# Running channel attention and SwiGLU in one loop, and moving a tile's closing sum ahead of the next row maxima

## The chip, the core and the metric

The kernel runs on one core of one Trainium2 chip. A core has five engines that each work through their own queue of instructions in order: TensorE (PE in the profile, with its weight loads as PEld), VectorE (DVE), ScalarE (ACT), GpSimd (POOL) and SyncE (SP), which here only issues transfers. They meet only at semaphores: an instruction that waits holds up everything behind it on its own engine. The metric is the device time of one execution in microseconds (us).

## The reference, cut to what matters

A decoder of four layers with three sublayers each. Only the first three sublayers are touched. `x` is 64 sequences of 64 tokens with 256 features, 4096 tokens in all; each sublayer is added to its input and normalized.

```python
x = layernorm(x + attn(x))            # first:  16 heads of 16, one key/value head, causal
x = layernorm(x + xattn(x, ctx, ctx)) # second: attention over channels
x = layernorm(x + ffn(x))             # third:  SwiGLU, hidden size 704

def xattn(q, k, v):                   # per sequence
    scaled = einsum('bsd,bse->bde', q, k) / 16
    attn = softmax(scaled, axis=1)
    return einsum('bde,bse->bsd', attn, v)

def ffn(x):                           # weights are integers: W = (wq - 128) * scale
    return (silu(x @ Wgate.T) * (x @ Wup.T)) @ Wdown.T
```

The other nine sublayers (attentions, a recurrence, quantized feed-forwards) follow in the same way and are not changed.

## The kernel before

**Tiles.** `x` stays on the core, in eight groups of four tiles of 128 tokens (two sequences a tile): `self.X[g][:, t, :]`. The context is there twice, by token (`cn`) and turned (`self.CT[g]`). Every product is in float32; the profile lists such a product as two MATMUL instructions.

**Order.** Each sublayer is a method called from `run`; a framework places the instructions of each engine and writes the semaphores. Inside `with self.tc.manual_schedule(engines=...)` the named engines keep the order in which the code issues their instructions; the other engines are placed freely. Weights come through a ring of eight buffers of 8 KB per partition (`self.weight`). PSUM, which holds the products, has eight banks, divided afresh by each sublayer.

**First sublayer, `l0_attn`.** A loop of 36 iterations over the 32 tiles, with the order of TensorE, ScalarE, VectorE and GpSimd written out. In iteration i:

- TensorE: the scores of tile i (`s`, onto a mask product), the values of tile i-3 (`ot`), one part of the next group's projections (`prepare`: turning, then keys and values, then two halves of the queries), the turned probabilities of tile i-2 (`pt`), and the output projection of tile i-3 (`o`, one PSUM bank).
- VectorE: the largest value of each row of tile i (`mx`), the subtraction, the row sums of tile i-1 (`sm`), their reciprocal, and then `ended` for tile i-4: add the output in PSUM to the input (`z`, line 605), and the statistics (606, 607). After a group's fourth tile `ended` also issues the reciprocal root, half on VectorE (228), half on GpSimd (230).
- GpSimd: the products of probabilities and reciprocals (565), and the input with bias for the next group (`xb`, 521).

**Second sublayer, `l0_xattn`.** A loop over 32 tiles; only TensorE's order is written out. Per tile: four score products on 64 rows each into a PSUM tile of two banks (`s`, three buffers), the largest values (686, 687), four exponentials that also give their sums (692), the reciprocal (696), the division folded into the values on GpSimd (`vt`, 702), and, two tiles later, four value products (712), the sum (713) and, for the fourth tile of a group, the layernorm, its last step on VectorE (267).

**Third sublayer, `l0_ffn`.** Integer weights are loaded into one ring buffer each and scaled into another (line 778). For each group: two transposes (`xt`), then six chunks of 128 hidden features (the last has 64): a gate and an up product of four MATMULs each (738), the SiLU on ScalarE (740), the product on VectorE (741); then for each of four tiles the down product over all six chunks (749), the sum (792), and at the end the layernorm. No engine's order is written out.

The SiLU and the exponential need different tables on ScalarE; the compiler puts an ACT_TABLE_LOAD in front of an activation whose table is not the one loaded.

Of the kernel before, what the change touches and what calls it, by code (L numbers as in the profile page):

```python
# [9 lines left out]
F32 = mybir.dt.float32  # L10
BF16 = mybir.dt.bfloat16
FP8 = mybir.dt.float8e4
I32 = mybir.dt.int32
# [5 lines left out]
P = 128  # L19
# [5 lines left out]
NEG_INF = -1.0e38  # L25
ROUND = 12582912.0
WCOLS = 2048
LAYERS = 8


class Linear:
# [164 lines left out]
class Decoder:  # L196
# [154 lines left out]
    def run(self, layers):  # L351
        tc, nc, ctx = self.tc, self.nc, self.ctx
        self.const = self.pool(ctx, "const", 1)
        self.smallp = self.pool(ctx, "small", 4)
        self.xpool = self.pool(ctx, "xpool", 1)
        self.ring = self.pool(ctx, "ring", 8)

        self.X, self.CT, self.l3_rows = [], [], []
        for g in range(self.n_groups):
            xg = self.xpool.tile([P, TG, D], F32, tag=f"x{g}", name=f"x{g}")  # L360
            self.load(xg, self.ins["x"][g * NTOK : (g + 1) * NTOK, :].rearrange("(t p) d -> p t d", p=P))
            self.X.append(xg)
# [86 lines left out]
    def l0_attn(self, ctx):  # L449
# [178 lines left out]
        with self.tc.manual_schedule(engines={E.PE, E.Activation, E.DVE, E.Pool}):  # L628
# [34 lines left out]
        self.load(cn, self.ins["ctx"][g * NTOK : (g + 1) * NTOK, :].rearrange("(t p) d -> p t d", p=P))  # L663
        return cn

    def l0_xattn(self, ctx):

        nc = self.nc  # L670
        wk = ctx.enter_context(self.tc.tile_pool(name="l0x", bufs=2, reuse_waits="tile"))
# [3 lines left out]
        groups, state = {}, {}  # L675

        def scores(g, t):
            x, cn = self.X[g], groups[g][0]
            ps = self.psum.tile([P, 2, 2, D], F32, tag="s", name="s", bufs=3)
            for e in range(2):  # L680
                for b in range(2):
                    nc.tensor.matmul(
# [6 lines left out]
            for b in range(2):  # L689
                for e in range(2):  # L690
                    i = 2 * b + e
                    nc.scalar.activation(
                        p[:, b, e, :], ps[:, b, e, :], AF.Exp, bias=nb[:, i : i + 1], scale=scale,
                        accum_out=sm[:, i : i + 1],
                    )
            nc.vector.reciprocal(sm, sm)
# [3 lines left out]
            sums = sm.rearrange("p (b e) -> p b e", b=2)  # L700
            for b in range(2):
                nc.gpsimd.tensor_tensor(
                    vt[:, b], src[:, b], sums[:, b].unsqueeze(2).broadcast_to([P, 2, S]), ALU.mult
                )
            return p, vt

        def values(g, t, p, vt):
            x, z = self.X[g], groups[g][1]
            ps = self.bank("o", tag="o", bufs=2)
            for e in range(2):  # L710
                for b in range(2):
                    nc.tensor.matmul(ps[half(b), :D], vt[:, b, e, :], p[:, b, e, :], start=e == 0, stop=e == 1)
            nc.vector.tensor_tensor(z[:, t, :], ps[:, :D], x[:, t, :], ALU.add)
            if t == TG - 1:
                self.layernorm(x, z)

        tiles = [(g, t) for g in range(self.n_groups) for t in range(TG)]
        n = len(tiles)
        with self.tc.manual_schedule(engines={mybir.EngineType.PE}):
            for i in range(n + 2):  # L720
                if i < n:
                    g, t = tiles[i]
                    if t == 0:
                        groups[g] = cns[g], wk.tile([P, TG, D], F32, tag="z", name="z")
                    state[i] = scores(g, t)
                if i >= 2:
                    values(*tiles[i - 2], *state.pop(i - 2))

    def gated(self, wk, xt, w_gate, w_up, n_hid):

        nc = self.nc
        hs = []
        for h0 in range(0, n_hid, P):
            n = min(P, n_hid - h0)
            pg, pu = self.bank("gate"), self.bank("up")
            for ps, w in ((pg, w_gate), (pu, w_up)):
                for c in range(2):
                    nc.tensor.matmul(ps[:n], w(c, h0, n), xt[:, c, :], start=c == 0, stop=c == 1)
            h = wk.tile([P, NTOK], F32, tag="hid", name="hid", bufs=10)
            nc.scalar.activation(h[:n], pg[:n], AF.Silu)  # L740
            nc.vector.tensor_tensor(h[:n], h[:n], pu[:n], ALU.mult)
            hs.append((h, n))
        return hs

    def down(self, hs, w_down, t):

        ps = self.bank("down", tag="acc", bufs=2)
        for i, (h, n) in enumerate(hs):
            self.nc.tensor.matmul(
                ps[:, :D], h[:n, t * P : (t + 1) * P], w_down(i, n), start=i == 0, stop=i == len(hs) - 1  # L750
            )
        return ps[:, :D]

    def l0_ffn(self, ctx):

        nc, ins = self.nc, self.ins
        wk = self.pool(ctx, "l0f", 2)
        HID = 704
        ws = []
        for name, scale, n, parts in (  # L760
            ("l0_wg", "l0_sg", HID, 2),
            ("l0_wu", "l0_su", HID, 2),
            ("l0_wd", "l0_sd", D, 6),
        ):
            sc = self.spread(wk, scale, n)
            raw, w = self.weight(name + "_q", I32), self.weight(name)
            cols = parts * n
            full = ins[name].shape[0] // P
            r3 = raw[:, :cols].rearrange("p (c n) -> p c n", c=parts)
            w3 = w[:, :cols].rearrange("p (c n) -> p c n", c=parts)  # L770
            self.load(r3[:, :full, :], ins[name][: full * P, :].rearrange("(c p) n -> p c n", p=P))
            blocks = [(slice(0, P), c) for c in range(full)]
            if full < parts:
                rest = slice(0, ins[name].shape[0] - full * P)
                self.load(r3[rest, full, :], ins[name][full * P :, :])
                blocks.append((rest, full))
            for rows, c in blocks:
                nc.vector.scalar_tensor_tensor(
                    w3[rows, c, :], r3[rows, c, :], -128.0, sc[rows], ALU.add, ALU.mult
                )  # L780
            ws.append(w3)
        wg, wu, wd = ws
        for g in range(self.n_groups):
            x = self.X[g]
            xt = self.transposed(x, wk, "xt")
            hs = self.gated(
                wk, xt, lambda c, h, n: wg[:, c, h : h + n], lambda c, h, n: wu[:, c, h : h + n], HID
            )
            z = wk.tile([P, TG, D], F32, tag="z", name="z")
            for t in range(TG):  # L790
                ps = self.down(hs, lambda i, n: wd[:n, i, :], t)
                nc.vector.tensor_tensor(z[:, t, :], ps, x[:, t, :], ALU.add)
            self.layernorm(x, z)

    def l1_attn(self, ctx):

# [1367 lines left out]
```

## Time and profile before

| | |
|---|---|
| time, median of 3 runs | 4535.5 us (4533.63 to 4536.48) |
| time of the profiled execution | 4529.3 us |
| its span, first to last instruction | 4527.5 us |
| busy share of the span: PE, DVE, ACT, POOL | 91%, 69%, 42%, 33% |
| mean granted TensorE clock | 0.967 |
| first sublayer, by its first and last TensorE instruction | about 5 to 247 us |
| second sublayer | 247.3 to 355.7 us |
| seam between second and third, until the first gate and up products are done | 355.7 to 371.3 us |
| third sublayer, from there to its last product | 371.3 to 637.6 us |
| fourth sublayer starts | 637.6 us |

Each row of the views below gives an engine, a line of the kernel, the operation, and what it writes and reads by the program's names. In the list of instructions in order of time the first two columns are the start and the duration in us, and the square bracket is how long the engine sat idle before it and what ended that. The view by stretches gives for each the length, then each engine's busy time with its number of instructions, then the granted clock, the share of the transfer engines and GB/s. A busy TensorE is counted from the start of a MATMUL to its modelled end, which overlaps with the next, so the pace of its work is read from the distance between starts.

### The profile page before, as it was taken

The numbers are of one execution on the slowest core, as the hardware profiler recorded it, in microseconds if no ns is written. First come the engines' busy times: TensorE is split into PE (matmuls) and PEld (weight loads), VectorE is DVE, ScalarE is ACT, GpSimd is POOL, SyncE is SP. The second block draws the span as 40 slices with busy tenths as digits, with TensorE's granted clock in tenths as the row PEclk, the third lists the DMA queues.
The fourth block names the chain that finished last, engine by engine and source line by source line (L and its number), as shares of the span: only waits on it lengthen the run. The fifth ranks groups of instructions, "written<-read, shape, count | busy, mean of one in ns | idle before, by whom it ended". The sixth has DMA issues, their size and how long they took to land. (4 is left out here: it accounts for less than half of the span.)

```text
span 4527.5 us, 73819 instructions
## 1 busy us (share of the span) xinstructions
PE 4123.3 (91%) x28808; PEld 2661.1 (59%) x28808; DVE 3113.5 (69%) x6262; ACT 1920.5 (42%) x3552; POOL 1476.0 (33%) x1498
## 2 busy tenths in 40 slices
PE   7879997989988999849999999999979999999898
PEld 5544555666665555525666666666646666666566
DVE  6774235888775577767777777777757677777676
ACT  4551123767623566534444444444423332233344
POOL 3431011142331111105555555555523333333111
PEclk9999997999999999969999999999989999999999
DMA  4001011333300000011111111111220000000000
GB/s 129 3 1 47 1 35 37 60 82 70 80 1 21 1 0 1 10 47 24 29 29 24 29 29 24 29 29 24 57 68 10 10 10 10 10 10 13 7 16 17
DMA packets 99684, 128.25 MB, mean 28 GB/s; under 512 B 14916, under 2 KB 72452, under 8 KB 97928
## 3 DMA queue, kind: packets, MB, share of 16 engines
q1 hardware_dynamic: 99336, 123.53, 10.9%
q8 instruction: 228, 3.74, 0.3%
q14 instruction: 120, 0.98, 0.1%
HBM read 61.87 MB, written 19.42 MB: 18 GB/s over the span
## 5 line engine op out<-in xcount | busy, mean ns | idle before, releaser
L230 POOL TENSOR_TENSOR hrq<-hrq,neg_half 128x4 f32<-128x4 f32 x256 | 270.9, 1058 | 510.0 <-DVE hrq L228 509.9
L230 POOL TENSOR_TENSOR rstd<-rstd,neg_half 128x4 f32<-128x4 f32 (+1 forms) x168 | 148.3, 883 | 798.9 <-DVE rstd L228 713.4
L1003 DVE TENSOR_REDUCE mc<-sq 128x2 f32<-128x512 f32 x512 | 317.0, 681 | 61.1 <-PE sk L1001 60.7
L1009 ACT ACTIVATE e<-sk 128x512 f32<-128x512 f32 x512 | 265.1, 605 | 111.1 <-PE sk L1001 110.2
L230 POOL TENSOR_TENSOR hrk<-hrk,neg_half 128x4 f32<-128x4 f32 x160 | 187.9, 1175 | 290.8 <-DVE hrk L228 280.4
L998 PE MATMUL sq<-l1x 32*128 32x256 f32 x2048 | 273.9, 405 | 2.0 <-DVE mc L1003 2.0
L1505 PE MATMUL p<-l3a_wq,xt 128*128 128x512 f32 x512 | 244.4, 600 | 9.9 <-DVE v L217 9.9
L1001 PE MATMUL sk<-l1x 32*128 32x256 f32 x2048 | 251.5, 391 | 0.2 <-DMA l1x<-l1x_m 0.2
L1505 PE MATMUL p<-l3x_wq,xt 128*128 128x512 f32 x512 | 235.7, 603 | 14.1 <-DVE k L1814 14.0
L1505 PE MATMUL p<-l3a_wk,xt 128*128 128x512 f32 x512 | 247.1, 605 | 0.0
L998 PEld LDWEIGHTS sq<-l1x 32*128 32x128 f32 x2048 | 207.9, 194 | 54.8 <-issue 23.1
L1895 PE MATMUL acc<-l3x_wo,yt 128*128 128x256 f32 x1024 | 238.0, 385 | 0.7 <-ACT yt L215 0.7
L1505 PE MATMUL p<-l3a_wv,xt 128*128 128x512 f32 x512 | 234.4, 600 | 0.8 <-DVE k L217 0.4
L1712 PE MATMUL acc<-l3a_wproj,yt 128*128 128x256 f32 x1024 | 232.4, 380 | 0.0
L1712 PEld LDWEIGHTS acc<-l3a_wproj,yt 128*128 128x128 f32 x1024 | 194.7, 191 | 53.0 <-issue 29.2
L1895 PEld LDWEIGHTS acc<-l3x_wo,yt 128*128 128x128 f32 x1024 | 189.3, 190 | 28.3 <-ACT yt L215 0.9
L1001 PEld LDWEIGHTS sk<-l1x 32*128 32x128 f32 x2048 | 187.7, 186 | 6.9 <-issue 2.5
L1505 PEld LDWEIGHTS p<-l3x_wq,xt 128*128 128x128 f32 x512 | 96.7, 195 | 125.4 <-issue 115.1
L1696 POOL TENSOR_TENSOR hry<-hry,neg_half 128x8 f32<-128x8 f32 x64 | 106.2, 1660 | 192.9 <-DVE hry L1692 192.9
L1806 ACT ACTIVATE sq<-q 128x512 f32<-128x512 f32 x128 | 80.7, 630 | 205.4 <-DVE q L1814 153.1
L236 PEld LDWEIGHTS qT<-ident,q 128*128 128x128 f32 x1024 | 119.1, 141 | 77.5 <-issue 64.5
L236 PEld LDWEIGHTS pt<-ident,s 128*128 128x128 f32 x768 | 93.4, 144 | 105.8 <-issue 65.4
(374 smaller groups left out, 10227.9 us busy)
## 6 DMA issues: line engine op xcount, KB each, us to landing
vs<-v SPq DMA_DIRECT2D x320, 128.0 KB
x<-in_x SPq DMA_DIRECT2D x8, 512.0 KB
ct<-in_ctxT SPq DMA_DIRECT2D x8, 512.0 KB
cn<-in_ctx SPq DMA_DIRECT2D x8, 512.0 KB
l1x<-in_ctx SPq DMA_DIRECT2D x128, 32.0 KB
l1x_x<-x SPq DMA_DIRECT2D x8, 512.0 KB
l1x<-l1x_x SPq DMA_DIRECT2D x128, 32.0 KB
l1x_r<-r SPq DMA_DIRECT2D x128, 32.0 KB
```

Source lines behind the costliest of these rows:

```text
L230: nc.gpsimd.tensor_tensor(out, out, self.neg_half[:, :n], ALU.pow)
L236: self.nc.tensor.transpose(ps[:, j * P : (j + 1) * P], blk, self.ident)
L998: nc.tensor.matmul(ps[:, n, :], x_[rows, j, part], c_[rows, j, :], start=True, stop=True)
L1001: nc.tensor.matmul(ps[:, n, :], c_[rows, j, part], x_[rows, j, :], start=True, stop=True)
L1003: nc.vector.tensor_reduce(mc[new % 2][:, ra + k, 2 * j : 2 * j + 2], ps, AX.X, ALU.max, negate=True)
L1009: nc.scalar.activation(es[rb + k], ps, AF.Exp, scale=scale)
L1505: self.nc.tensor.matmul(ps, lhs(c), w(c, cols), start=c == 0, stop=c == 1 and bias is None)
L1696: nc.gpsimd.tensor_tensor(r, r, self.neg_half[:, :8], ALU.pow)
L1712: nc.tensor.matmul(acc[:, :D], yts[h % 2][:, h // 2, :], wp[n // 8][:, (n % 8) * D : (n % 8 + 1) * D], start=n == 0, stop=n == 15,)
L1806: nc.scalar.activation(sq, x, AF.Square)
L1895: nc.tensor.matmul(acc[:, :D], yts[h % 2][:, h // 2, :], wo[n // 8][:, (n % 8) * D : (n % 8 + 1) * D], start=n == 0, stop=n == 15,)
```

## The change

Two things change.

In `l0_attn`, `ended` for tile i-4 moves from behind the row sums of tile i-1 to the head of the iteration, in front of the scores and row maxima of tile i.

`l0_xattn`, `l0_ffn` and their helpers `gated` and `down` are replaced by one method, `l0_both`, with the order of all four compute engines written out. Its loop runs over 48 units, one per group and chunk of the third sublayer, with eight units ahead and two behind. Unit u issues the gate and up products of chunk u, the scores of a tile of the second sublayer (of the next group; in four of six units), the down products of chunk u-2 for all four tiles, and the values of the tile whose scores came two units earlier. Scores fall on units with u mod 6 = 4, 5, 0, 1 and values on u mod 6 = 0, 1, 2, 3; the next group's rows are turned at the end of units with u mod 6 = 5. Its statistics are taken tile by tile, and the normalization is applied on ScalarE instead of VectorE, one unit after the last sum. PSUM: `s` has one buffer of two banks instead of three, `o` one bank, gate, up and the turned rows share three, and the accumulators have two. Integer weights are scaled in place, so three ring buffers are taken instead of six.

```diff
@@ run
-            self.l0_attn, self.l0_xattn, self.l0_ffn, self.l1_attn, self.l1_both,
+            self.l0_attn, self.l0_both, self.l1_attn, self.l1_both,
@@ l0_attn
             for i in range(n + 4):
                 behind = ends.pop(0) if ends else None
+                if i >= 4:
+                    ended(*tiles[i - 4], state.pop((i - 4, "ps")))
                 if i < n:
...
                 if 3 <= i <= n + 2:
                     state[i - 3, "o"] = values(*tiles[i - 3], state.pop((i - 3, "pt")))
-                if i >= 4:
-                    ended(*tiles[i - 4], state.pop((i - 4, "ps")))
                 if parts:
                     parts.pop(0)()
@@ l0_both
-    def l0_xattn(self, ctx):
...
-    def gated(self, wk, xt, w_gate, w_up, n_hid):
...
-    def down(self, hs, w_down, t):
...
-    def l0_ffn(self, ctx):
...
+    def l0_both(self, ctx):
...
+            raw = self.weight(name, I32)
+            r3 = raw[:, : parts * n].rearrange("p (c n) -> p c n", c=parts)
+            w3 = raw.bitcast(F32)[:, : parts * n].rearrange("p (c n) -> p c n", c=parts)
...
+        def ended(g, z):
+            mv = state.pop((g, "mv"))
+            rstd, nb = self.small(TG, "rstd", bufs=4), self.small(TG, "nmr", bufs=4)
+            self.rsqrt(rstd, mv[:, :, 1], 1.0, 1e-5)
+            def apply():
+                nc.vector.scalar_tensor_tensor(nb, mv[:, :, 0], -1.0, rstd, ALU.mult, ALU.mult)
+                for i in range(TG):
+                    nc.scalar.activation(
+                        self.X[g][:, i, :], z[:, i, :], AF.Identity, bias=nb[:, i : i + 1], scale=rstd[:, i : i + 1]
+                    )
+            ends.append(apply)
+        def sums(g, t, z, ps):
...
+            nc.vector.tensor_tensor(z[:, t, :], ps, self.X[g][:, t, :], ALU.add)
+            nc.vector.bn_stats(st, z[:, t, :])
+            nc.vector.bn_aggr(state[g, "mv"][:, t, :], st)
...
         def scores(g, t):
...
-            ps = self.psum.tile([P, 2, 2, D], F32, tag="s", name="s", bufs=3)
+            ps = self.psum.tile([P, 2, 2, D], F32, tag="s", name="s", bufs=1)
...
+        def divided(g, t):
+            p, sm = state[g, t]
             nc.vector.reciprocal(sm, sm)
...
+        def values(g, t):
...
+            sums(g, t, z, ps[:, :D])
             if t == TG - 1:
-                self.layernorm(x, z)
+                ended(g, state.pop((g, "z")))
...
+        def turn(g):
+            xt = wk.tile([P, 2, NTOK], F32, tag="xt", name="xt")
+            for c, copy in enumerate((nc.scalar.copy, nc.vector.tensor_copy)):
+                ps = self.bank("xt", tag="gu", bufs=3)
+                for t in range(TG):
+                    nc.tensor.transpose(ps[:, t * P : (t + 1) * P], self.X[g][:, t, c * P : (c + 1) * P], self.ident)
+                copy(xt[:, c, :], ps)
...
+        def hidden(g, i):
+            pg, pu = self.bank("gate", tag="gu", bufs=3), self.bank("up", tag="gu", bufs=3)
...
+            nc.scalar.activation(h[:n], pg[:n], AF.Silu)
             nc.vector.tensor_tensor(h[:n], h[:n], pu[:n], ALU.mult)
...
+        def down(g, i):
...
+            for t in range(TG):
+                nc.tensor.matmul(
+                    state[g, "acc"][t // 2][:, t % 2, :], h[:n, t * P : (t + 1) * P], wd[:n, i, :],
+                    start=i == 0 and t % 2 == 0, stop=i == HC - 1, skip_group_check=True,
                 )
+            if i < HC - 1:
+                return
...
+            for t in range(TG):
+                sums(g, t, z, acc[t // 2][:, t % 2, :])
+            ended(g, z)
+        tiles = [(g, t) for g in range(self.n_groups) for t in range(TG)]
+        units = [(g, i) for g in range(self.n_groups) for i in range(HC)]
+        at = {HC * (g - 1) + t - 2: (g, t) for g, t in tiles}
+        E = mybir.EngineType
+        with self.tc.manual_schedule(engines={E.PE, E.Activation, E.DVE, E.Pool}):
+            for u in range(min(at), len(units) + 2):
+                behind = ends.pop(0) if ends else None
+                if 0 <= u < len(units):
+                    hidden(*units[u])
+                if behind:
+                    behind()
+                if u - 1 in at:
+                    divided(*at[u - 1])
+                if u in at:
+                    scores(*at[u])
+                if u >= 2:
+                    down(*units[u - 2])
+                if u - 2 in at:
+                    values(*at[u - 2])
+                if (u + 1) % HC == 0 and (u + 1) // HC < self.n_groups:
+                    turn((u + 1) // HC)
+            for part in ends:
+                part()
```

More of the change, by code (lines that the diff above doesn't have):

```diff
@@ L27 @@
 WCOLS = 2048
-LAYERS = 8
+LAYERS = 7
 class Linear:
@@ L664, in context @@
         return cn
-    def l0_xattn(self, ctx):
-        nc = self.nc
-        wk = ctx.enter_context(self.tc.tile_pool(name="l0x", bufs=2, reuse_waits="tile"))
+    def l0_both(self, ctx):
+        nc, ins = self.nc, self.ins
+        HID = 704
+        HC = (HID + P - 1) // P
+        wk = ctx.enter_context(self.tc.tile_pool(name="l0b", bufs=2, reuse_waits="tile"))
         cns = [self.context(g) for g in range(self.n_groups)]
@@ L674, in l0_xattn @@
         scale = 1.0 / 16.0
-        groups, state = {}, {}
+        ws = []
+        for name, sc_name, n, parts in (
+            ("l0_wg", "l0_sg", HID, 2),
+            ("l0_wu", "l0_su", HID, 2),
+            ("l0_wd", "l0_sd", D, HC),
+        ):
+            sc = self.spread(wk, sc_name, n)
+            raw = self.weight(name, I32)
+            full = ins[name].shape[0] // P
+            r3 = raw[:, : parts * n].rearrange("p (c n) -> p c n", c=parts)
+            w3 = raw.bitcast(F32)[:, : parts * n].rearrange("p (c n) -> p c n", c=parts)
+            self.load(r3[:, :full, :], ins[name][: full * P, :].rearrange("(c p) n -> p c n", p=P))
+            blocks = [(slice(0, P), c) for c in range(full)]
+            if full < parts:
+                rest = slice(0, ins[name].shape[0] - full * P)
+                self.load(r3[rest, full, :], ins[name][full * P :, :])
+                blocks.append((rest, full))
+            for rows, c in blocks:
+                nc.vector.scalar_tensor_tensor(
+                    w3[rows, c, :], r3[rows, c, :], -128.0, sc[rows], ALU.add, ALU.mult
+                )
+            ws.append(w3)
@@ new lines, in l0_both @@
+        wg, wu, wd = ws
+        state, ends = {}, []
+        def ended(g, z):
[7 more added lines that the diff above has]
+                        self.X[g][:, i, :], z[:, i, :], AF.Identity, bias=nb[:, i : i + 1], scale=rstd[:, i : i + 1]
+                    )
+            ends.append(apply)
@@ L677, in scores @@
+        def sums(g, t, z, ps):
+            if t == 0:
+                state[g, "mv"] = self.smallp.tile([P, TG, 2], F32, tag="bnmv", name="bnmv", bufs=4)
+            st = self.smallp.tile([P, 6], F32, tag="bnst1", name="bnst1", bufs=4)
+            nc.vector.tensor_tensor(z[:, t, :], ps, self.X[g][:, t, :], ALU.add)
+            nc.vector.bn_stats(st, z[:, t, :])
+            nc.vector.bn_aggr(state[g, "mv"][:, t, :], st)
         def scores(g, t):
-            x, cn = self.X[g], groups[g][0]
@@ L679, in scores @@
-            ps = self.psum.tile([P, 2, 2, D], F32, tag="s", name="s", bufs=3)
+            x, cn = self.X[g], cns[g]
+            if t == 0:
+                state[g, "z"] = wk.tile([P, TG, D], F32, tag="z", name="z", bufs=3)
+            ps = self.psum.tile([P, 2, 2, D], F32, tag="s", name="s", bufs=1)
             for e in range(2):
@@ L695, in scores @@
                     )
+            state[g, t] = p, sm
+        def divided(g, t):
+            p, sm = state[g, t]
             nc.vector.reciprocal(sm, sm)
@@ L699, in scores @@
             src = self.CT[g][:, :, t * P : (t + 1) * P].rearrange("p e (b s) -> p b e s", b=2)
-            sums = sm.rearrange("p (b e) -> p b e", b=2)
+            sums_ = sm.rearrange("p (b e) -> p b e", b=2)
             for b in range(2):
                 nc.gpsimd.tensor_tensor(
-                    vt[:, b], src[:, b], sums[:, b].unsqueeze(2).broadcast_to([P, 2, S]), ALU.mult
+                    vt[:, b], src[:, b], sums_[:, b].unsqueeze(2).broadcast_to([P, 2, S]), ALU.mult
                 )
[L705 to L709, printed above, removed]
+            state[g, t] = p, vt
+        def values(g, t):
+            p, vt = state.pop((g, t))
+            ps = self.bank("o", tag="o", bufs=1)
             for e in range(2):
@@ L712, in values @@
                     nc.tensor.matmul(ps[half(b), :D], vt[:, b, e, :], p[:, b, e, :], start=e == 0, stop=e == 1)
-            nc.vector.tensor_tensor(z[:, t, :], ps[:, :D], x[:, t, :], ALU.add)
+            z = state[g, "z"]
+            sums(g, t, z, ps[:, :D])
             if t == TG - 1:
-                self.layernorm(x, z)
[L717 to L727, printed above, removed]
@@ L729, in gated @@
-    def gated(self, wk, xt, w_gate, w_up, n_hid):
[L731 to L736, printed above, removed]
+                ended(g, state.pop((g, "z")))
[6 more added lines that the diff above has]
+                copy(xt[:, c, :], ps)
+            state[g, "xt"] = xt
@@ L737, in gated @@
+        def hidden(g, i):
+            xt, h0 = state[g, "xt"], i * P
+            n = min(P, HID - h0)
+            pg, pu = self.bank("gate", tag="gu", bufs=3), self.bank("up", tag="gu", bufs=3)
+            for ps, w in ((pg, wg), (pu, wu)):
                 for c in range(2):
-                    nc.tensor.matmul(ps[:n], w(c, h0, n), xt[:, c, :], start=c == 0, stop=c == 1)
-            h = wk.tile([P, NTOK], F32, tag="hid", name="hid", bufs=10)
+                    nc.tensor.matmul(ps[:n], w[:, c, h0 : h0 + n], xt[:, c, :], start=c == 0, stop=c == 1)
+            h = wk.tile([P, NTOK], F32, tag="hid", name="hid", bufs=4)
@@ L740, in gated @@
             nc.scalar.activation(h[:n], pg[:n], AF.Silu)
             nc.vector.tensor_tensor(h[:n], h[:n], pu[:n], ALU.mult)
-            hs.append((h, n))
-        return hs
-    def down(self, hs, w_down, t):
[L747 to L752, printed above, removed]
-    def l0_ffn(self, ctx):
[L756 to L779, printed above, removed]
-                )
[L781 to L789, printed above, removed]
-            for t in range(TG):
-                ps = self.down(hs, lambda i, n: wd[:n, i, :], t)
-                nc.vector.tensor_tensor(z[:, t, :], ps, x[:, t, :], ALU.add)
-            self.layernorm(x, z)
@@ new lines, in hidden @@
+            state[g, "h", i] = h, n
+        def down(g, i):
+            h, n = state.pop((g, "h", i))
+            if i == 0:
+                state[g, "acc"] = [
+                    self.psum.tile([P, 2, D], F32, tag="acc", name="acc", bufs=2) for _ in range(2)
+                ]
+            for t in range(TG):
+                nc.tensor.matmul(
+                    state[g, "acc"][t // 2][:, t % 2, :], h[:n, t * P : (t + 1) * P], wd[:n, i, :],
+                    start=i == 0 and t % 2 == 0, stop=i == HC - 1, skip_group_check=True,
+                )
+            if i < HC - 1:
+                return
+            acc = state.pop((g, "acc"))
+            z = wk.tile([P, TG, D], F32, tag="z", name="z", bufs=3)
+            for t in range(TG):
+                sums(g, t, z, acc[t // 2][:, t % 2, :])
+            ended(g, z)
```

## The prediction

> **What bounds the kernel now.** I read the busy times by stretches first, one stretch per sublayer and seam.
>
> ```profile
> 46.00:216.00 170.00, 144.91 (x2201) 99.97 (x2185) 134.05 (x191) 91.83 (x156) 73.21 (x72) 1.00 0.02 3
> 216.00:247.30 31.30, 23.15 (x370) 17.53 (x369) 22.12 (x37) 14.37 (x27) 10.04 (x6) 0.84 0.01 2
> 247.30:355.70 108.40, 80.69 (x513) 46.22 (x512) 81.52 (x229) 62.94 (x260) 32.33 (x72) 0.96 0.00 1
> 355.70:371.30 15.60, 10.78 (x34) 6.04 (x34) 7.35 (x14) 3.05 (x4) 1.96 (x2) 0.71 0.67 196
> 371.30:637.60 266.30, 264.83 (x801) 138.45 (x799) 91.64 (x195) 31.54 (x53) 9.91 (x10) 1.00 0.05 17
> ```
>
> The third sublayer (last row) is TensorE end to end, with ScalarE at 12%; the second has no full engine: a chain. In the first, TensorE and VectorE are both nearly full, so I went to the waits of 0 to 247 us, then to the instructions in order of time.
>
> ```profile
> DVE mx L553 <- PE s L544: 56.2, 26, 9.2
> PE o L595 <- DVE z L605: 21.6, 22, 2.8
> ```
> ```profile
> 147.12 0.36 DVE L605 TENSOR_TENSOR z<-o,xb 128x256 f32<-128x256 f32 x1
> 147.53 1.13 PE L595 MATMUL o<-l0a,ot 128*128 128x256 f32 x4 [0.41 <-DVE z L605]
> 149.03 0.69 PE L544 MATMUL s<-kbd,qT 32*64 32x128 f32 x32
> 149.83 1.22 DVE L553 TENSOR_REDUCE mx<-s 128x16 f32<-128x1024 f32 x1 [1.67 <-PE s L544]
> ```
>
> Each waits for the other: `o` has one PSUM bank and starts only when `z` has read it; the next scores lie behind `o`; the next maxima wait for them; and `z` is last in VectorE's iteration.
>
> **Edit 1, `ended` first.** Nothing is added; three or four VectorE instructions move past four others, and once per group the root (230) moves past a product (565) on GpSimd. No transfer moves. In the new order `z` starts when the previous `o` is done, 1.15 after its start, and its three steps take 0.39+0.46+0.18 = 1.03 by their starts, so VectorE is free 2.2 after the start of `o`; scores are ready for it at 2.3 (149.83-147.53). So `mx` is not delayed, and `o` finds its bank free. In a steady group the waits for `z` are 0.41, 0.47 and 1.22 (the fourth iteration, with keys and values, takes 7.85 and has none): 2.1, in six groups 12.6, and 1.35 in the first iteration that has one. The last tiles have no projections; there the waits are 2.82, 2.82 and 1.93, but VectorE's own iteration is 4.85 (1.26+1.14+1.24+0.18 and the 1.03) against TensorE's 3.8, so about 1.2 of each stays: 4 saved. Those gaps also halve the clock from 229 to 242 (`o` to `o` takes 8.5 there instead of 6.6); I take 3 for that. Sum -21. Late next is TensorE itself; a smaller wait is the root's first half (228): it took 1.75 at 127.31 while `xb` ran on GpSimd, 0.16 alone, and now stands in front of `mx`: 0 to 0.7 per group, and I take 0. The scaling of the weights (line 778, 1.7+1.7+2.1 = 5.5 of VectorE) loses its cover: its scales wait for memory of the first sublayer, so it falls into that drain or the next start, at 0 to 5.5; VectorE is 70% busy there, and I take 2. **First part: -19.**
>
> **Edit 2, the two sublayers together.** Before, from the first score to the last down product: 637.6-247.3 = 390.3.
>
> *TensorE's work in the loop.* The paces:
>
> ```profile
> 469.55 1.88 PE L738 MATMUL up<-xt,l_wu 128*128 128x512 f32 x4
> 471.27 1.88 PE L738 MATMUL gate<-xt,l_wg 128*128 128x512 f32 x4
> 259.72 1.13 PE L682 MATMUL s<-x,cn 64*128 64x256 f32 x8
> 260.78 1.17 PE L712 MATMUL o<-p,vt 128*64 128x256 f32 x8
> 261.88 0.49 PE L682 MATMUL s<-x,cn 64*128 64x256 f32 x2
> ```
>
> Gate and up take 1.72 each, so 20.6 a group and 0.24 for the narrow chunk. Down takes 2.98 per tile now (z at 460.49, 463.47), which is twelve at 0.213 and 0.21 for each change to and from the 64-row chunk; that chunk now comes once for all tiles, so 48 x 0.216 + 0.4 = 10.8 instead of 11.9. Scores and values take 1.06 + 1.10 a tile next to each other; between other shapes each change costs about 0.2 more, so 2.47, or 9.9 a group. Turning takes 1.0. Sum 42.5 a group.
>
> *What waits.* Scalar work has moved between the SiLUs: a unit with a tile runs SiLU, table, four exponentials, table. The closest rows are in a later stage, where the same two functions alternate:
>
> ```profile
> 1555.53 0.47 ACT L1309 ACTIVATE wv<-qk,ss 128x256 f32<-128x256 f32 x1
> 1556.02 1.28 ACT L1339 ACT_TABLE_LOAD   x1
> 1557.31 0.60 ACT L1339 ACTIVATE hid<-gate 128x512 f32<-128x512 f32 x1
> ```
>
> A switch is 1.31 there. 26 units of the loop have both, so 53 switches, 69 us of ScalarE. Walking the four queues through a group: in most units they fit under TensorE's 7.4 (3.43 + 1.27 + 1.73 down + 1.0 or more of values): from SiLU, 0.6, product 0.8, reciprocal 0.17, maxima 1.45, exponentials 1.95, table 1.3, that is 6.3 until the next SiLU may start. The exception is the turn of the rows. In unit 4 of the group the four normalizations (2.1) stand in front of the first tile's exponentials, and unit 5 has no values to cover it. From the product in unit 4 at 0: normalized 2.4, table 3.7, exponentials 5.6, table 6.9, SiLU 7.6, product 8.4, reciprocal and maxima 10.0, exponentials 12.0, and only then ScalarE's copy of the turned rows, 12.6. TensorE is through its turning at 9.8: a wait of 2.8, where now it is 0.3. What waits behind it: the next group's first gate, and all TensorE work. Groups 0 to 5: 42.5+2.8, say 45.5 with a hop or two; less 3.5 as the first two units have no down. Group 6 has two score sets less and only 0.7 of that wait, 40.7; group 7 has no tiles, 31.6; the two units behind, 3.9. Loop: 6 x 45.5 - 3.5 + 40.7 + 31.6 + 3.9 = 345.7.
>
> *The units ahead.* Eight units have no chunk: group 0's tiles run alone, and with one `s` buffer a tile's scores wait for the previous exponentials. A tile is then scores 1.1 (1.9 at half clock), maxima 1.45, exponentials 1.95, hops: 5.3. The first ends at 6.8, as the last normalization of sublayer one is in front; three more, 22.7; reciprocal, `vt`, values, sum, root (1.4) and normalizing, 8, 30.6; the next group's first two tiles' exponentials are queued in front of the copy of turned rows, 7.9: 38.5 all at half clock, 33 at full clock. At 254.69 and 256.55 these products took 1.93 and 2.08 after a gap of 5; I take 36, and 2 for first gates at half clock (3.75 instead of 1.88 for four at 364.53). In unit -7 the test for turning is also true, for group -1: eight transposes of the last group's rows that nobody reads. They fall into a wait and cost nothing, or 1 to 2 if that cover is gone.
>
> Together 38 + 345.7 = 383.7 instead of 390.3: -6.6. The seam's 15.6, and its wait for weights (four loads now in the first 50 us, unless the transfers of `vs` are held up, at most 4), are in that sum.
>
> *The end.* Now the last sum follows its product, and the fourth sublayer starts 4.1 later, when the memory is free. After: four sums 4.1 from the last product, root 1.4, normalizing 2.1 on ScalarE instead of 1.4 on VectorE: 7.5. +3.4. The reductions for the fourth sublayer (L817, L818, 3.7 each) and the clears of its successor run under the third now; they find VectorE half busy, or fall behind the loop, where their result is needed 20 us later: 0, at most 4.
>
> **Sum.** -19 - 6.6 + 3.4 = -22.2. The profiled execution took 4529.3, which is 6.2 under the median; it would take 4507, and the median becomes 4513.
>
> **A rule against it.** The rows say 1.31 per switch. The Trainium skill ("ScalarE: Activation LUTs", What ACT_TABLE_LOAD costs, and the rules at its end) asks for activations batched by table, and for 2.66 per switch, as 1.38 of drain comes on top of the load. In the row SiLU starts 0.01 after the load. With its number the unit's chain is 7.7, over TensorE's 7.4, and the wait at each turn grows by 3.1; seven turns make +22 and the sum is nothing. I take the row, as it is the same pair of functions.
>
> **The rivals.** 0.2% (9 us) is what a measurement here tells from no change.
>
> *Forecast*, 0.50: 4500 to 4526.
>
> *More comes of it*, 0.20: 4492. The clock stays full ahead of the loop (-4), the turn's wait is half of seven times 2.8 (-9), and the first sublayer loses its waits of 0.3 to 0.5 for other parts too (-8). For it: an undisturbed TensorE is at 1.00 through 46 to 216 us.
>
> *The ring closes again or the table costs what the rule says*, 0.16: 4532. `mx` then waits behind `z`, which waits for `o`, with a margin of 0.1 only, and edit 1 is worth its drain alone, -3; the chain of the other case ends at the same time.
>
> *Slower: the chain from SiLU to SiLU paces the units*, 0.14: 4556. My 6.3 has hops of 0.1 in few places; VectorE also runs sums[...] (1.22 for a nominal 0.16 at 133.80), and each link is in order. It decides from 7.4 a unit; at 9.0, 26 units lose 1.6 each, 42 us. For it: ScalarE's waits for `nb` in the second sublayer, 38.4, show how late that link is even with three buffers. Against it: the later stage with the same pair keeps TensorE at 94 to 97%.
>
> The range leaves out most of the slower case and little below: 4486 to 4540. Faster by over 0.2%: the forecast almost whole, and the one under it, 0.70; same 0.16; slower 0.14.
>
> **What would show it.** `o` should no longer wait for `z` in 46 to 216 us, and that sublayer end near 228. ACT_TABLE_LOAD in front of the SiLU and the exponential, some 53 times at 1.28. A group of the loop near 45.5, with one wait of 2 to 4 of the first gate for ScalarE's copy. First gate about 36 after the first score. Wrong: gates waiting for `hid` or scores for `p` in each unit (the slower case), or a first sublayer as long as now.

## The result, and the profile after

The change takes 4524.7 us, the median of 16 runs, against 4535.6 of the kernel before in the runs beside it: 10.8 us less, a ratio of 0.9974 with a 95% interval of 0.9966 to 0.9982. The forecast was 4513. The total hides two larger numbers of opposite sign: the new order in the first sublayer gains far more than forecast, and the merged stage loses where a small gain was forecast.

| stretch, profiled executions | before | after | difference | forecast |
|---|---|---|---|---|
| start to the second sublayer's first score | 247.3 | 219.4 | -27.9 | -21 |
| first score to the last down product | 390.3 | 400.0 | +9.7 | -6.6, and 2 for the weights' scaling |
| last product to the fourth sublayer's first keys | 4.8 | 7.6 | +2.8 | +3.4 |
| whole execution | 4529.3 | 4522.9 | -6.4 | -22.2 |

The last product is taken by the start of the fourth sublayer's first turned row, which follows it on TensorE. The first three rows make -15.4. What comes back after them is looked at below; part of it is that the profiled execution of before was 6 us under that kernel's median, the one of after 2 us.

**First sublayer.** Instructions of the changed kernel in order of time, one steady iteration (start, duration, engine, what it does):

```profile
133.38 0.66 PE L236 MATMUL pt<-ident,s 128*128 128x128 f32 x4 [0.34 <-ACT qT L530]
133.88 1.03 PE L595 MATMUL o<-l0a,ot 128*128 128x256 f32 x4
135.27 0.69 PE L544 MATMUL s<-kbd,qT 32*64 32x128 f32 x32
```
```profile
134.95 0.42 DVE L605 TENSOR_TENSOR z<-o,xb 128x256 f32<-128x256 f32 x1 [0.76 <-PE o L595]
135.41 0.43 DVE L606 BATCH_NORM_STATS2 bnst<-z 128x6 f32<-128x256 f32 x1
135.87 0.18 DVE L607 BATCH_NORM_AGGREGATE bnmv<-bnst 128x2 f32<-128x6 f32 x1
136.09 0.20 DVE L228 TENSOR_SCALAR rstd<-bnmv 128x4 f32<-128x4 f32 x1
136.19 1.21 DVE L553 TENSOR_REDUCE mx<-s 128x16 f32<-128x1024 f32 x1
```

Nothing stands in square brackets in front of `o`: its bank is free. `z` starts 1.07 after `o`, and the maxima follow without a pause. VectorE now waits for TensorE (the view of waits, 46 to 216 us):

```profile
DVE z L605 <- PE o L595: 22.0, 20, 3.1
```

**The merged loop.** The view by stretches, one row from the first score to the first gate and one for each of the groups 0 to 2, then group 7 with the two units behind (length, busy times of the five engines, granted clock, DMA share, GB/s):

```profile
219.39:260.58 41.19, 19.70 (x98) 11.81 (x97) 21.83 (x48) 16.49 (x59) 7.03 (x12) 0.69 0.11 28
260.58:309.37 48.79, 43.85 (x152) 22.47 (x153) 22.69 (x37) 24.12 (x52) 4.99 (x10) 0.87 0.16 47
309.37:354.96 45.59, 41.94 (x169) 22.68 (x169) 18.85 (x47) 26.20 (x56) 5.05 (x10) 1.00 0.00 1
354.96:402.19 47.23, 43.57 (x169) 23.32 (x169) 19.61 (x48) 26.20 (x56) 5.94 (x11) 0.96 0.01 4
583.90:619.44 35.54, 35.54 (x112) 20.32 (x113) 9.46 (x23) 5.65 (x10) 1.01 (x1) 1.00 0.17 57
```

| part | forecast | measured |
|---|---|---|
| first score to first gate, and what the first gate and up products lose at half clock | 38 | 41.2 and 2.8 |
| group 0, without that loss | 42.0 | 46.0 |
| groups 1 to 5 | 227.5 | 233.0 |
| group 6 | 40.7 | 41.5 |
| group 7 and the units behind | 35.5 | 35.5 |
| sum | 383.7 | 400.0 |

Three causes stand in the trace. First the turn of the rows, once a group. ScalarE, VectorE and TensorE in front of group 2's first gate:

```profile
348.40 0.59 ACT L797 ACTIVATE hid<-gate 64x512 f32<-64x512 f32 x1
351.20 1.28 ACT L748 ACT_TABLE_LOAD   x1 [2.21 <-DVE nb L743]
352.50 0.47 ACT L748 ACTIVATE p<-s,nb 128x256 f32<-128x256 f32 x1
...
354.31 0.59 ACT L786 COPY xt<-xt 128x512 f32<-128x512 f32 x1
```
```profile
350.93 0.17 DVE L743 TENSOR_SCALAR nb<-nb 128x4 f32<-128x4 f32 x1
```
```profile
350.27 1.04 PE L785 MATMUL xt<-ident,x 128*128 128x128 f32 x8
354.96 3.62 PE L795 MATMUL gate<-xt,l_wg 128*128 128x512 f32 x4 [3.65 <-ACT xt L786]
```

TensorE has turned the rows at 351.3 and sits idle for 3.65, because the copy stands behind four exponentials, those behind a table load, and that load starts only when the maxima are there (351.1), though ScalarE has been idle for 2.21. And the gate after the gap takes 3.62 instead of 1.98: the clock is at half. This is what tells the 47.2 row from the 45.6 row (0.96 against 1.00); four of the five gaps of 3.65 are followed by it.

Second, in the stretch up to the first gate, VectorE does the weights' scaling, 5.9 us, in front of the second tile's maxima:

```profile
226.04 0.18 DVE L757 RECIPROCAL sm4x<-sm4x 128x4 f32<-128x4 f32 x1 [2.61 <-ACT p L748]
226.13 1.88 DVE L698 SCALAR_TENSOR_TENSOR l_wg<-l_wg,l_sg 128x704 f32<-128x704 int32 x2
227.94 1.89 DVE L698 SCALAR_TENSOR_TENSOR l_wu<-l_wu,l_su 128x704 f32<-128x704 int32 x2
229.75 2.08 DVE L698 SCALAR_TENSOR_TENSOR l_wd<-l_wd,l_sd 128x256 f32<-128x256 int32 x6
231.76 1.21 DVE L742 TENSOR_REDUCE nb<-s 128x4 f32<-128x1024 f32 x1
```

Third, in group 0 the fourth sublayer's reductions have moved in (their weights load early now), and the second one holds up a tile's sum; nine us later that is a wait of the scores for exponentials, and these scores run at half clock:

```profile
288.87 3.68 DVE L869 TENSOR_REDUCE l1a<-l_wo 128x256 f32<-128x2048 f32 x1 [2.98 <-DMA l_wo<-in_l_wo]
292.47 0.42 DVE L725 TENSOR_TENSOR z<-o,x 128x256 f32<-128x256 f32 x1
```
```profile
301.55 2.08 PE L738 MATMUL s<-x,cn 64*128 64x256 f32 x8 [3.52 <-ACT p L748]
```

The table loads themselves are as forecast, 53 at 1.283 us (groups of ScalarE between 219 and 620 us; busy time in us and the mean in ns, then idle time before them):

```profile
L797 ACT ACT_TABLE_LOAD x27 | 34.6, 1283 | 0.5
L748 ACT ACT_TABLE_LOAD x26 | 33.4, 1283 | 61.5 <-DVE nb L743 59.2 <-PE gate L795 2.2
```

The second row is what matters: the loads for SiLU run ahead of their data, those for the exponentials sit behind it, 59.2 us of waiting for `nb` in front of them.

### The profile page after: what moved, and what is told of

The parts are those of the page before. It is cut to its first block, busy times and chain, and to the rows that moved or that the text cites. A ratio compares the mean times of both kernels' runs of the same rounds, so it can differ in the third digit from the quotient of the medians.

```text
span 4521.2 us, 73893 instructions
## 1 busy us (share of the span) xinstructions
PE 4119.8 (91%) x28796; PEld 2664.4 (59%) x28816; DVE 3089.4 (68%) x6215; ACT 2020.6 (45%) x3669; POOL 1477.0 (33%) x1498
## 5 line engine op out<-in xcount | busy, mean ns | idle before, releaser
L1088 PE MATMUL ret<-e,vt 128*32 128x256 f32 x2048 | 140.0, 389 | 17.5 <-DVE mc L1054 16.6
```

What stands on the lines that cost most here:

```text
L1088: nc.tensor.matmul(ret[32 * r : 32 * r + 32, :], vt[i % 2][:, lc, 4 * r + j, :], es[r][:, lc, :], start=lc == 0, stop=lc == 1,)
```

## The experiments

Times are medians of four to seven executions unless said otherwise; the ratio is to the kernel before, run beside them. That kernel took 4538.3 beside the first four experiments, 4535.9 beside the next three and 4534.2 beside the last two, so a difference between kernels of different sets has some 3 us of play.

**Each edit alone.** Edit 1 alone is the kernel before with

```diff
                 behind = ends.pop(0) if ends else None
+                if i >= 4:
+                    ended(*tiles[i - 4], state.pop((i - 4, "ps")))
...
-                if i >= 4:
-                    ended(*tiles[i - 4], state.pop((i - 4, "ps")))
                 if parts:
```

> Edit 1 alone, in the kernel before. Theory (the parts add up, and what the change loses it loses in the merged stage): the first sublayer ends near 219 instead of 247, the second and third sublayers keep their 390 from first score to last product, and the whole is some 28 us under the kernel before, 17 under the change, but for up to 8 us either way by which gaps of later stages the clock gate catches. Rival (edit 1 only moves work: the gain of 28 in the first sublayer comes back as a later start of something behind it, so the merged stage is not what loses): the second sublayer starts 28 earlier and takes that much longer, and the whole is 10 us or less under the kernel before.

Measured: 4505.9 us, 0.9932 (0.9920 to 0.9945), 32 us less than before. The first score comes at 219.9, and the stretch from there to the last product is 391.1. Its rival falls: nothing of the gain comes back in the second sublayer.

Edit 2 alone is the changed kernel with those two lines at their old place.

> Edit 2 alone: the merged stage behind the first sublayer in its old order. Theory: first score at 247, from there to the last product 400 instead of 390, the end 3.6 longer: about 13 us slower than the kernel before, but for up to 8 us by the clock gate in later stages. Rival (the merged stage is as good as the prediction had it, 6.6 less, and suffers only from the first sublayer's shorter drain): first score to last product 384 and the whole 3 us or more faster than before.

Measured: 4554.7 us, 1.0039 (1.0026 to 1.0053), 16 us slower than before. First score at 246.6, and 400.5 from there to the last product. So the merged stage loses whatever stands in front of it, and the two edits add up within their intervals: -32 and +16 against the -11 of both. By edit 1 alone the kernel is 19 us faster than by the change (22 by the distances from before).

**The scaling of the weights, one unit after the other.**

```diff
+                if scaled and u > min(at):
+                    scaled.pop(0)()
```

Each `scaled` entry is one weight's scaling, issued behind a unit's `scores`.

> The change, with the scaling of the three SwiGLU weights issued on VectorE one by one behind the maxima of the second, third and fourth unit ahead of the loop, instead of in front of the second tile's maxima. Theory (those 5.9 us of VectorE stand on the chain of the units ahead): the first gate comes 5 to 6 us earlier after the first score (36 instead of 41), and the whole is 5 us faster than the change, but for the clock gate. Rival (the weights' transfers or GpSimd set the pace there): the first gate stays at 40 or later.

Measured: 4524.0 us, no difference to the change. The first gate came 40.3 after the first score, not 36. That is the rival's number, but not for its reason: the third tile's scores do come 3.6 earlier, but the third scaling stands in front of a tile's sum, and `o` waits for that sum (VectorE and TensorE of this kernel):

```profile
239.22 2.09 DVE L700 SCALAR_TENSOR_TENSOR l_wd<-l_wd,l_sd 128x256 f32<-128x256 int32 x6
241.24 0.41 DVE L729 TENSOR_TENSOR z<-o,x 128x256 f32<-128x256 f32 x1
```
```profile
241.79 1.97 PE L776 MATMUL o<-p,vt 128*64 128x256 f32 x8 [2.36 <-DVE z L729]
```

**The turn.** The exponentials are split off `scores` and issued behind `turn`; no instruction is added, TensorE's order stays.

```diff
                 if (u + 1) % HC == 0 and (u + 1) // HC < self.n_groups:
                     turn((u + 1) // HC)
+                if u in at:
+                    exponentials(*at[u])
```

> The change, with a tile's exponentials issued on ScalarE behind the copy of the turned rows (in the units with a turn), instead of in front of it. TensorE's order is the same. Theory (the turn waits because the table load, the four exponentials and the copy are in one line): the wait of a group's first gate falls from 3.65 to under 0.5, that gate runs at 1.98 instead of 3.62, a group takes 40.5 instead of 45.6, the loop 30 us less, and the whole 25 to 32 us less than the change. Rival (the chain from SiLU to SiLU is the limit, and the wait only moves): the exponentials come later, the next unit's scores wait for them by the 3 us saved, and a group stays within 1.5 us of 45.6.

Measured: 4490.3 us, 0.9900 (0.9886 to 0.9913), 34 us less than the change (37 by the distances from before). The same place of the loop in this kernel, ScalarE and then TensorE in order of time:

```profile
347.97 0.59 ACT L790 COPY xt<-xt 128x512 f32<-128x512 f32 x1 [1.91 <-PE xt L789]
348.57 1.28 ACT L752 ACT_TABLE_LOAD   x1
```
```profile
347.33 1.04 PE L789 MATMUL xt<-ident,x 128*128 128x128 f32 x8
348.60 1.98 PE L799 MATMUL gate<-xt,l_wg 128*128 128x512 f32 x4 [0.24 <-ACT xt L790]
```

The wait is 0.24, every first gate but the very first runs at 1.98, and each of the groups 1 to 5 takes 42.17. The rival falls: the exponentials come later, and TensorE waits for nothing in groups 1 to 6 but 0.24 for the copy, once a group. So the SiLU-to-SiLU chain is not what paces a unit. A group of 40.5 was too hopeful: 45.59 less 3.65 is 41.9.

**The table load by itself.** To the change, behind each SiLU whose unit has a tile, one exponential of a single column of constants:

```diff
             nc.scalar.activation(h[:n], pg[:n], AF.Silu)
+            if HC * g + i in at:
+                junk = self.small(1, "junk")
+                nc.scalar.activation(junk, self.neg_half[:, :1], AF.Exp)
```

> The change, with one exponential of a single column of constants behind each SiLU whose unit has a tile, so that the exponential's table is loaded while ScalarE would wait for the maxima. Theory (the load stands on the chain of the turn, between maxima and exponentials): the wait of a group's first gate falls from 3.65 by 1.3 to 2.3 or 2.4, a steady group at full clock from 45.6 to 44.3. Rival (the load runs ahead of the maxima already, or what ends the wait is another thing): the wait stays at 3.6.

Measured, in a single execution: 4501.3 us. The load now runs while the maxima are made (ScalarE and TensorE of this kernel):

```profile
345.69 1.28 ACT L800 ACT_TABLE_LOAD   x1
346.98 0.20 ACT L800 ACTIVATE junk<-neg_half 128x1 f32<-128x1 f32 x1
348.19 0.47 ACT L748 ACTIVATE p<-s,nb 128x256 f32<-128x256 f32 x1 [1.01 <-DVE nb L743]
```
```profile
350.66 1.98 PE L795 MATMUL gate<-xt,l_wg 128*128 128x512 f32 x4 [1.25 <-ACT xt L786]
```

The wait of groups 2 to 6 falls by 2.4, nearly twice what was expected, since two loads stood on that chain: the one in unit 5 and the one behind the four normalizations of unit 4. A gap of 1.25 leaves the clock alone, so a group takes 43.19.

**Scaling and reductions in better places**, both on top of the exponentials behind the turn. `folds` holds the two reductions.

```diff
+                if u - min(at) in (0, 1, 6):
+                    scaled.pop(0)()
...
+                if u - HC * (self.n_groups - 1) in (1, 3):
+                    folds.pop(0)()
```

> The kernel with the exponentials behind the turn, and the scaling of the weights put where VectorE sits idle: gate weights behind the first tile's maxima, up weights behind the second's, down weights behind the first maxima of the next group. Theory (placed behind the maxima of tiles that have sums to do, as in the run with the scaling later, the 5.9 us only moved in front of those sums, so the chain kept them): first gate 34 to 35 after the first score instead of 40, the whole 5 us less than with the exponentials behind the turn alone. Rival (the units ahead are set by scores, maxima and exponentials, and the scaling is hidden): first gate still at 39 to 40.

> The kernel with the exponentials behind the turn, and the two reductions of the fourth sublayer's output weights (3.7 us of VectorE each, now between 277 and 290 us) issued in the last group's units, which have no tile. Theory (the second reduction delays the sums of group 1's last tile, hence its normalization, the exponentials behind it and the scores of the next unit, which then wait 3.7 and run at half clock): group 0 of the loop takes 39 to 40 us instead of 45.9, the whole 5 to 6 us less. Rival (the first group is long because SiLU and exponentials have just begun to alternate): group 0 stays at 45 or 46.

> Both: scaling in the gaps and reductions in the last group, with the exponentials behind the turn. If the parts add up, first score to last product is 360 to 361 us instead of 372, and the whole is 10 to 11 us less than with the exponentials behind the turn alone, near 4480. If the later stages take it back by the clock gate, it is 4485 or more.

Measured: scaling in the gaps 4487.0 (first gate 36.2 after the first score, instead of 39.7; 34 to 35 was expected), reductions in the last group 4487.1 (group 0 takes 39.2 instead of 45.9), both 4481.3, a ratio of 0.9877 (0.9862 to 0.9892). In the trace the first takes 3.5 off the way to the first gate and 2.0 off group 0, where less time falls on half clock (4.2 us instead of 7.5); the second takes 6.8 off group 0. Together the stretch from first score to last product is 361.3, as added up beforehand. In the medians they are worth 3.4 and 3.3, together 9. This is the fastest kernel of the study, 55 us under before and 43 under the change. Its stretches up to the first gate, of group 0 and of group 1:

```profile
217.40:253.68 36.28, 20.28 (x98) 11.86 (x97) 20.70 (x48) 14.68 (x51) 5.79 (x12) 0.72 0.12 32
253.68:292.48 38.80, 38.36 (x152) 19.74 (x153) 14.59 (x34) 22.83 (x51) 4.03 (x9) 1.00 0.09 28
292.48:334.65 42.17, 41.93 (x168) 22.69 (x168) 18.60 (x48) 26.30 (x56) 5.04 (x10) 1.00 0.00 1
```

TensorE is busy for 41.9 of 42.2; the 36 us ahead of the loop are what is left.

**The seam to the fourth sublayer.** Two casts of constants stood there. Before, the mask's cast started 0.06 ahead of three GpSimd additions and took 0.42; in the change it starts 0.05 behind the first of them and takes 2.58 (VectorE and GpSimd, first before, then the change):

```profile
641.78 0.42 DVE L825 CAST mask<-same 128x512 bf16<-128x512 f32 x1
```
```profile
641.84 7.17 POOL L840 TENSOR_TENSOR xb<-x,l_bo 128x1024 f32<-128x1024 f32 x3 [1.65 <-DVE x L267]
```
```profile
626.58 2.58 DVE L876 CAST mask<-same 128x512 bf16<-128x512 f32 x1
629.08 0.68 DVE L889 COPY xt<-xt 128x512 f32<-128x512 f32 x1
```
```profile
626.53 7.13 POOL L891 TENSOR_TENSOR xb<-x,l_bo 128x1024 f32<-128x1024 f32 x3 [2.50 <-ACT x L714]
```

The first edit issues both casts with the second reduction; the second one also normalizes two of the last group's four tiles on VectorE.

```diff
         def both():
+            nc.vector.tensor_copy(ident, self.ident)
+            nc.vector.tensor_copy(mask, self.same.unsqueeze(1).broadcast_to([P, TG, P]))
             fold(half, raw[1])
```

> The kernel with scaling in the gaps and reductions in the last group, and also the fourth sublayer's two casts of constants (identity and mask to bf16) issued on VectorE with the second reduction, instead of behind the third sublayer. Theory (in the change the mask's cast starts 0.05 us behind a GpSimd addition of 7.1 us and takes 2.58 instead of 0.42, and the copy of turned rows stands behind it): the fourth sublayer's first keys come 5.2 to 5.6 us after the first turned row instead of 7.6, and the whole is 2 us less. Rival (the end's loss also sets where later gaps fall for the clock gate): from the first turned row of the fourth sublayer to the last key score of the fifth it takes 576 us as in the kernel with edit 1 alone, instead of 584, and the whole is 8 us less.

> The same, and the last group of the merged stage is normalized by two engines, two tiles on VectorE and two on ScalarE, instead of four on ScalarE. Theory: 2.07 becomes 1.1, so the first keys come another 1 us earlier and the whole is 1 us less, which five rounds can hardly tell. Rival as for the casts: the place in the clock's grid changes the later stages by up to 8 us either way.

Measured: 4483.8 and 4483.7, not to be told from the 4481.3 without them. The first keys still come 7.6 after the first turned row: ScalarE's copy of the first half ends that wait, so the expectation had the wrong engine. The cast had delayed the second half, and there 1.7 is saved (the keys and values of the first group take 6.3 instead of 8.0). With the normalizing split the first keys come at 6.7, 1.0 earlier as expected. Neither shows in the total, nor in the stretch from the fourth sublayer's first turned row to the fifth's last key score: 582.3 and 582.0, where the rival expected 576.

**A second profile of the kernels with separate sublayers**, one execution each.

> The kernel before once more, for a second profile. In its first profile the stretch from the fourth sublayer's first turned row to the fifth's last key score took 572.6 us, in ten profiles of kernels with the merged stage 580 to 585. The clock changes on a grid of 3.41 us that lay differently against the program's start in each profile. Theory (that first profile, 6 us under the kernel's median, was a lucky place in the grid): 575 to 579 here. Rival (the merged stage loses 8 us or more to what comes behind it): 573 or less again.

> Edit 1 alone once more, for a second profile of the same stretch, which took 575.8 us in its first. Theory as for the kernel before (separate sublayers 574 to 579, merged ones 580 to 585, so a loss of some 6, of which 3.6 lie in the first 8 us). Rival (no difference but luck): 580 or more.

Measured for that stretch: 579.3 and 576.8 (whole executions: 4540.4 and 4509.5). With 572.6 and 575.8 of the first profiles the separate kernels have a mean of 576.1, the eight merged ones with the casts in their old place 580.3 to 585.2, mean 583.3. So the merged stage does lose 7 us behind its last product, and the 11.7 that the first two profiles show (584.3 against 572.6) was partly the luck of one execution. Of the 7, 2.8 lie before the first keys and up to 1.7 in the cast, though taking the cast and 1.0 of the 2.8 away left the stretch at 582. The rest goes with time at half clock: 65 to 75 us of that stretch in the four separate profiles, 78 to 92 in the merged. Why the waits of unchanged code fall so much more often on a half-clock stretch there was not found.

## Why the prediction was right or wrong

The direction and the range held, but with luck: two errors partly cancelled. Edit 1 was forecast at -21 and measured -32 by itself; edit 2, with the scaling and the end, was forecast at -1.2 and measured +16.

- **Edit 1, the ring of `o` and `z`: right mechanism, gain too small.** The wait is gone and the margin of 0.1 held. Mis-sized is the 2.1 per group: a steady group went from 27.47 to 23.76, 3.71 in all. The prediction added the idle times listed in front of `o`. Such a time counts from the modelled end of the product before, which an `o` that waits for nothing overlaps, so the distance between starts is what tells. Before (the `o` behind this row stands in the prediction, at 147.53):

```profile
146.47 0.66 PE L236 MATMUL pt<-ident,s 128*128 128x128 f32 x4 [0.34 <-ACT qT L530]
```

From this `pt` to `o` it is 1.06, where 0.41 was listed; in the change it is 0.50 (133.38 to 133.88), so the wait cost 0.56. All four iterations of a group shrank by more than what was listed, by 0.6 to 1.7 (6.60 to 5.86 where 0.47 was listed). The fourth, booked as having no wait, had one of 0.41 for `v`, whose addition stood behind `z` on VectorE: 7.85 became 7.12. Six groups of 1.6 more are 9.7; the first iterations and the drain gave 2.8 less than forecast, so the first score came 6.9 earlier than forecast.
- **The root in front of the maxima (228) at 0: right.** It takes 0.20 in five groups of seven, 0.55 in one and 1.10 in the drain; the steady groups all take 23.76.
- **The weights' scaling, 2 of 0 to 5.5:** 3.4 by the median of its run. VectorE was half idle there, but the scaling stood in the chain from scores to exponentials.
- **TensorE's work, 42.5 a group:** 41.9. Right.
- **53 table loads at 1.28: right,** and the 2.66 of the Trainium skill ("ScalarE: Activation LUTs", What ACT_TABLE_LOAD costs) is not what counts here: 46 of the 53 activations start 0.01 behind their load, and taking two loads off the chain took 2.4 off the wait, 1.2 each.
- **The wait at the turn, 2.8: the step that failed is the walk through ScalarE's queue.** Its list goes from maxima at 10.0 to exponentials at 12.0 with no load between, as if the table were loaded while ScalarE waits. The rows show the load behind the wait for `nb`. The wait was 3.65, and the half clock at the first gate behind it, 1.7, four times in five, was not in the sum at all.
- **First gate 36 after the first score:** 41.2. Moving the scaling, which the prediction put at 2 and ahead of the first score, takes 3.5 off it. The queue of exponentials in front of the copy, another 1.5, was in the sum. The cause of the other 1.7 is not shown.
- **The eight transposes that nobody reads: right.** They start at 228.07, and the scores behind them still wait 5.24 for exponentials.
- **The fourth sublayer's reductions at 0, at most 4: failed.** They cost 6.8 in group 0 by the trace, 3.3 by the median. VectorE was indeed half busy there, but the chain ran through it.
- **The end, +3.4:** +2.8. Right; the cast's 1.7 was not foreseen, nor the half clock behind it.
- **The rivals:** the slower one, a SiLU-to-SiLU chain that paces each unit, did not happen: no gate waited for `hid`, scores waited for `p` six times and not in each unit, all before 302 us, and putting the exponentials later cost nothing. That edit 2 alone makes the kernel slower is still true, through a wait once a group instead of in each unit.

## What to carry to other kernels

When two functions alternate on ScalarE, ask for each table load what it is queued behind: here a load in front of an instruction that waits for another engine came after that wait, until something issued earlier pulled it forward. What feeds the next stage of TensorE (here a copy of turned rows) belongs ahead of work that has a unit's time to spare. And when a stage becomes one long chain, what moves into it from its neighbours (here the scaling and the reductions) can stand on the path, however idle its engine looks on average. When a small wait is priced, read it from the distance between starts, before and after, and not from the idle time listed.

## What the runs showed of the hardware

The granted clock moves on a grid. In all fourteen traces half-clock stretches last 3.41 us or a multiple, but for the last one of a trace, and the grid lies at phases from 0.2 to 3.4 us against the program's start, as the Trainium skill has it ("TensorE: Matmul & The Clock Gate", Part 1: a free-running window of 3413 ns).

The skill's advice to keep idle gaps under 3 us (the table "Why this matters for your kernels" on that page) is not safe here. In the change and the two other kernels with that wait (edit 2 alone, the scaling moved by units), the gaps of 3.65 were followed by half clock twelve times in fifteen; the five of 1.25 never were. In between, gaps of 2.20, 2.21 and 2.61 in front of group 1's first gate were, in all three kernels that have one; one of 2.16 in front of group 0's first gate (edit 2 alone) was not. The last of the three, in the kernel with the table loaded early (TensorE):

```profile
305.77 3.28 PE L795 MATMUL gate<-xt,l_wg 128*128 128x512 f32 x4 [2.61 <-ACT xt L786]
```

Even shorter ones can be. In the fifth sublayer a gap of 1.54 and one of 0.27 behind it were followed by half clock in the change (the products after it start 0.42 apart instead of 0.21), and not in the kernel before, where the same rows stand (first the change, then before; the third row of each is a product after the gap):

```profile
868.21 0.33 PE L1066 MATMUL mt<-ident,mc 128*128 128x128 f32 x1 [1.54 <-DVE mc L1054]
868.81 1.07 PE L1088 MATMUL ret<-e,vt 128*32 128x256 f32 x16 [0.27 <-DVE mc L1054]
871.69 0.99 PE L1049 MATMUL sq<-l1x 32*128 32x256 f32 x2
```
```profile
880.04 0.33 PE L1015 MATMUL mt<-ident,mc 128*128 128x128 f32 x1 [1.54 <-DVE mc L1003]
880.64 1.07 PE L1037 MATMUL ret<-e,vt 128*32 128x256 f32 x16 [0.27 <-DVE mc L1003]
883.05 0.56 PE L998 MATMUL sq<-l1x 32*128 32x256 f32 x2
```

For a cast on VectorE beside an addition on GpSimd, the order of their starts decided. The cast of 128x512 from fp32 to bf16 took 0.42 with GpSimd idle (the two kernels with the casts moved), and 0.42 in the four profiles where it started 0.05 to 0.06 ahead of an addition, which then took 2.57 instead of 2.34. In the eight where it started 0.05 behind the addition it took 2.58 and ended 0.3 after it.
